# A second copy of the first weight, loaded in 2 KB pieces, for the first 16 batches of a conditional adapter

## The chip, the cores and the metric

The kernel runs on one core of one Trainium2 chip. The metric is the time of one launch on the device, in microseconds (us), as the median of several runs. A profile of one further execution stands beside it.

## What is computed

`x` is 128 batches of 128 x 512 float32. Every batch has an id that picks one of ten sets of adapter weights: W1 (512 x 128), b1, W2 (128 x 512), b2, gamma and beta. The reference, cut to what matters:

```python
w1 = W1[language_ids]; w2 = W2[language_ids]
h = relu(einsum('bsh,bha->bsa', x, w1) + b1[ids][:, None, :])
adapted = einsum('bsa,bah->bsh', h, w2) + b2[ids][:, None, :]
y = x + adapted
normed = (y - mean(y)) * rsqrt(var(y) + 1e-5)          # over the last axis, 512
out = x + normed * gamma[ids][:, None, :] + beta[ids][:, None, :]
```

## The kernel before

All ten W1 and all ten W2 are loaded into SBUF once (2.62 MB each) and stay there; a batch picks its own by a register that holds its id. `x` comes in groups of four batches (`load_x`, 1 MB, four buffers), results leave in pairs (`store`, 512 KB). All large transfers are issued by SyncE (SP) in one order; an instruction that waits holds up those behind it on SP. Every engine's order is written out by hand: `keep` ties each instruction to the one before it on its engine.

One batch `b` takes these steps:

- `transpose_x(b)` (L199): four TensorE transposes turn the 128 x 512 block into four 128 x 128 blocks in PSUM. Column block `k` of `x` holds the 128 consecutive columns from `k * 128`. The block of `x` is the stationary operand of the transpose, so it is read by the weight load (LDWEIGHTS, "PEld" in the profile); the identity matrix streams past it.
- `copy_xT(b)` (L204): ScalarE (ACT) copies the result to SBUF.
- `stage_w1(b)` (L194): ACT copies the batch's W1 from the resident table `w1` to a small buffer `w1s`[...].
- `down(b)` (L221): four matmuls, each over 128 of the 512 columns, give h transposed in the one PSUM buffer `ph`; they show as eight records.
- `relu(b)` (L231): ACT adds b1, applies relu and writes `hT`; it frees `ph` for `down(b + 1)`.
- `up(b)` (L235): a matmul with W2, 512 wide, into one of five PSUM buffers `py`. For batches 0 to 3 and some others one more matmul (L241) adds b2 there.
- VectorE (DVE) adds x (`residual`) and later scales (`scale`, `finish`), ACT squares and takes the deviation, GpSimd (POOL) forms x + b2 (`add_b2`, tile `r`) and x + beta (`add_beta`, tile `o`, five pair buffers).

In the main loop TensorE does, for each `i`, `transpose_x(i)`, `down(i - 1)`, `up(i - 2)`.

Ahead of that loop stands a start-up. SP issues: the ids, gamma, x of batches 0 and 1 (`load_part`, L84), W1 in four transfers (L98), x of batches 2 and 3, W2 in two transfers (L103), x of batches 4 to 7 in two, then groups 2 and 3 (`load_x`, L67). Each of the four W1 transfers brings the rows of one column block `k` of all ten sets: to a partition go ten separate pieces of 128 floats, 512 bytes each. W2 and `x` come in 2 KB pieces.

Meanwhile thirty rows (ten each of beta, gamma, b2) are spread over all partitions: `spread(r)` is a matmul on TensorE (L163) and a copy of its result from PSUM by DVE (L168) or ACT (L166), even rows on DVE and odd ones on ACT. Rows 0 to 23 come before the first `stage_w1`; rows 24 to 29 come in a loop over the first four batches (called the four-batch loop here), which also holds `down(0)` to `down(3)`, `transpose_x(2)` and `(3)`, the relus, and `stage_w1(2)` to `(5)`. `spin` is filler work on TensorE. After the four-batch loop come `up(0)` and `up(1)`, the first use of W2.

Of the kernel before, what the change touches and what calls it, by code (L numbers as in the profile page):

```python
# [8 lines left out]
FP = mybir.dt.float32  # L9
# [4 lines left out]
ET = mybir.EngineType  # L14
PSUM = bass.MemoryType.PSUM

P = 128
G = 4
EPS = 1e-5
U = 2  # L20


@with_exitstack
def cond_resid_kernel(ctx: ExitStack, tc: tile.TileContext, x, itok, W1, b1, W2, b2, gamma, beta, out):
# [8 lines left out]
    nc = tc.nc  # L33
    B, S, H = x.shape
    L, _, A = W1.shape
    KC = H // P
# [6 lines left out]
    def keep(ins):  # L43

        engine = ins.ins.engine
        if engine in last:
            tc.add_manual_dep(ins.ins, last[engine], behind, reason="kept order")
        last[engine] = ins.ins.name
        return ins

    const = ctx.enter_context(tc.tile_pool(name="const", bufs=1))
# [13 lines left out]
    def load_x(g):  # L65
        t = xp.tile([P, G, H], FP, tag="x", name=f"x_{g}")
        keep(nc.sync.dma_start(out=t, in_=x[g * G : (g + 1) * G].rearrange("b s h -> s b h")))  # L67
        xs[g] = t

    def xb(b):  # L70
        return xs[b // G][:, b % G, :]
# [3 lines left out]
    rows = rp.tile([P, H], FP, tag="r", name="rows")  # L75
    b1r = const.tile([L, A], FP, name="b1r")
    w1 = const.tile([P, L, KC, A], FP, name="w1")
    w2 = const.tile([P, L * H], FP, name="w2")
    x_0 = xp.tile([P, G, H], FP, tag="x", name="x_0")
    xs[0] = x_0  # L80

    def load_part(lo, hi):
        dst = xs[lo // G][:, lo % G : lo % G + hi - lo, :]
        keep(nc.sync.dma_start(out=dst, in_=x[lo:hi].rearrange("b s h -> s b h")))  # L84
# [8 lines left out]
    warm = const.tile([P, 1], FP, name="warm")  # L93
    keep(nc.vector.memset(warm, 1.0))
    keep(nc.scalar.activation(warm, warm, AF.Sqrt))
    for k in range(KC):
        keep(
            nc.sync.dma_start(out=w1[:, :, k, :], in_=W1[:, k * P : (k + 1) * P, :].rearrange("l p a -> p l a"))  # L98
        )
    load_part(2, G)  # L100
    for l in range(0, L, 5):
        keep(
            nc.sync.dma_start(  # L103
                out=w2[:, l * H : (l + 5) * H].rearrange("p (l h) -> p l h", l=5),
                in_=W2[l : l + 5].rearrange("l a h -> a l h"),
# [3 lines left out]
    xs[1] = x_1  # L109
    load_part(G, G + 2)  # L110
    load_part(G + 2, 2 * G)
    for g in range(2, 4):
        load_x(g)

    ident = const.tile([P, P], FP, name="ident")
    make_identity(nc, ident)
    eps = const.tile([P, 1], FP, name="eps")
    nc.gpsimd.memset(eps, EPS)
    ones = const.tile([P, P], BF, name="ones")
# [4 lines left out]
    R = 3 * L  # L124
# [34 lines left out]
    def spread(r, copier):  # L159
        t = (beta_b, gamma_b, b2_b)[r // L]  # L160
        row = p_y.tile([P, H], FP, tag="y", name=f"row_{r}")
        pick_r = pick[:, r : r + 1].to_broadcast([96, P])
        keep(nc.tensor.matmul(row, lhsT=pick_r, rhs=parts[:96, :], start=True, stop=True))  # L163
        dst = t[:, r % L * H : (r % L + 1) * H]
        if copier is nc.scalar:
            keep(nc.scalar.copy(dst, row))  # L166
        else:
            keep(nc.vector.tensor_copy(dst, row))  # L168

    lids, xT, w1s, hT, rs, os, ys, ssqs, nmeans, rstds = {}, {}, {}, {}, {}, {}, {}, {}, {}, {}  # L170
    phs, pxs, sums = {}, {}, {}

    def lid(b, engine):
        g = b // G
        if (g, engine) not in lids:
            loads, vals = nc.values_load_multi_w_load_instructions(
                lang[0:1, g * G : (g + 1) * G],
                engines=[engine],
                min_val=0,
                max_val=L - 1,  # L180
                skip_runtime_bounds_check_because="clamped on the chip to 0..L-1 above",
            )
            for ins in loads:
                keep(ins)
            lids[g, engine] = vals
        return lids[g, engine][b % G]
# [6 lines left out]

    def stage_w1(b):  # L194
        w1s[b] = wp.tile([P, KC, A], FP, tag="w1s", name=f"w1s_{b}")
        src = w1.rearrange("p l k a -> p (l k a)")[:, bass.ds(lid(b, ET.Activation) * (KC * A), KC * A)]
        keep(nc.scalar.copy(w1s[b].rearrange("p k a -> p (k a)"), src))  # L197

    def transpose_x(b):  # L199
        pxs[b] = p_x.tile([P, KC, P], FP, tag="xT", name=f"pxT_{b}")  # L200
        for k in range(KC):
            keep(nc.tensor.transpose(pxs[b][:, k, :], xb(b)[:, k * P : (k + 1) * P], ident))  # L202

    def copy_xT(b):  # L204
        xT[b] = tp.tile([P, KC, P], FP, tag="xT", name=f"xT_{b}")
        keep(nc.scalar.copy(xT[b], pxs.pop(b)))  # L206
# [14 lines left out]
    def down(b):  # L221
        phs[b] = p_h.tile([P, P], FP, tag="h", name=f"ph_{b}")
        for k in range(KC):
            keep(
                nc.tensor.matmul(  # L225
                    phs[b], lhsT=w1s[b][:, k, :], rhs=xT[b][:, k, :], start=(k == 0), stop=(k == KC - 1)
                )
            )
        del xT[b], w1s[b]

    def relu(b):  # L231
        hT[b] = tp.tile([P, P], FP, tag="hT", name=f"hT_{b}", bufs=6)
        keep(nc.scalar.activation(hT[b], phs.pop(b), AF.Relu, bias=b1T[:, bass.ds(lid(b, ET.Activation), 1)]))  # L233
# [53 lines left out]
    def rstd_1(g):  # L287
        y0s[g] = p_s.tile([P, 6], FP, tag="s", name=f"stat_{g}")
        keep(nc.vector.reciprocal(y0s[g][:, 0:2], sds[g]))  # L289

    def rstd_2(g):
        t = y0s[g]
        keep(nc.vector.scalar_tensor_tensor(t[:, 2:4], ssqs.pop(g), EPS * H3, t[:, 0:2], ALU.add, ALU.mult))

# [27 lines left out]
    def on(b):  # L322
        return 0 <= b < B
# [6 lines left out]
    def rstd_of(b, n):  # L330
# [6 lines left out]
        elif n == 2:  # L337
            keep(
                nc.vector.scalar_tensor_tensor(t[:, 1:2], ssqs.pop(b), EPS * H3, t[:, 0:1], ALU.add, ALU.mult)
            )  # L340
# [94 lines left out]
    def spin(n, width):  # L435
        idle = p_s.tile([P, H], FP, tag="s", name="idle")
        for _ in range(n):
            keep(
                nc.tensor.matmul(
                    idle[:, :width], lhsT=ones, rhs=ones[:, 0:1].to_broadcast([P, width]), start=True, stop=True  # L440
                )
            )


    def spread_turn(lo, hi):
        for r in range(lo, hi):
            spread(r, nc.scalar if r % 2 == 1 else nc.vector)
            if r % 2 == 1:
                spin(1, H // 2)
# [6 lines left out]
    spread_turn(2, 8)  # L456
    transpose_x(1)
    copy_xT(1)
    spread_turn(8, 24)
    stage_w1(0)  # L460
    stage_w1(1)
    spin(3, H)
    for b in range(4):
        down(b)
        if b < 2:
            transpose_x(b + 2)
        relu(b)
        if b < 2:
            copy_xT(b + 2)
        for r in range(24 + 2 * b, min(26 + 2 * b, R)):  # L470
            spread(r, nc.scalar if r % 2 == 1 else nc.vector)
        stage_w1(b + 2)
    up(0)
    up(1)

    for i in range(3, B + U):
        b = i - U - 1
        if b > 0 and b % G == 0 and b // G + 3 < NG:
            load_x(b // G + 3)
        if i == 4:  # L480
            up(2)
        if i == 5:
            up(3)
        if i > 3 and on(i):
            transpose_x(i)
        if b <= E:
            add_b2(b + 2)
            add_beta(b)
        if i > 4 and on(i - 1):
            down(i - 1)  # L490
        if i > 3 and on(i):
            copy_xT(i)
        if i > 4 and on(i + 1):
            stage_w1(i + 1)
        if i > 4 and on(i - 1):
            relu(i - 1)
        if i > 5 and on(i - U):
            up(i - U)


        g, half = divmod(b, 2)
        p = g - 1
        mine, old = 0 <= p < B // 2, 0 <= p - 1 < B // 2
        if b == E:
            add_b2(b + 3)
            add_beta(b + 1)
            add_b2(b + 4)
            for n in range(b + 2, B):
                add_beta(n)
        if b > E:  # L510
            tail(b)
        elif half == 0:
            if on(b):
                residual(b)
            if mine:
                rstd_1(p)
                scale(2 * p)
            if on(b):
                negative_mean(b)
            if mine:  # L520
                rstd_2(p)
            if old:
                finish(2 * p - 1)
                store(p - 1)
            if mine:
                rstd_3(p)
        else:
            if on(b):
                residual(b)
            if mine:  # L530
                rstd_4(p)
                scale(2 * p + 1)
            if on(b):
                negative_mean(b)
            if mine:
                finish(2 * p)
        if 0 <= b <= E:
            square(b)
            if half == 1:
                deviation(g)  # L540

        for n, engine in ((i + 3, ET.Activation), (i - U + 3, ET.PE), (b + 1, ET.DVE), (b + 5, ET.Pool)):
            if on(n):
                lid(n, engine)
# [37 lines left out]
```

## Time and profile before

| quantity | value |
|---|---|
| median of 3 runs | 314.34 us (314.3 to 314.67) |
| the profiled execution's own time | 314.2 us |
| its span in the profile | 312.4 us |
| TensorE (PE) busy | 300.3 us, 96% |
| DVE, ACT, POOL busy | 295.6, 285.8, 280.1 us |
| moved by DMA | 72.87 MB, 233 GB/s over the span |

The span runs from the first to the last instruction of the program; 1.8 us of the execution's time lie outside it. "Busy" is the time in which an engine has an instruction in flight. In the tables of the profile a group is named by line, engine, operation and tiles (output first, then inputs), and "issue" is time in which an engine waited for nothing that the profile shows. The 40 slices are 7.8 us each; a digit is the busy share in tenths.

### The profile page before, as it was taken

The numbers are of one execution on the slowest core, as the hardware profiler recorded it, in microseconds if no ns is written. First come the engines' busy times: TensorE is split into PE (matmuls) and PEld (weight loads), VectorE is DVE, ScalarE is ACT, GpSimd is POOL, SyncE is SP. The second block draws the span as 40 slices with busy tenths as digits, with TensorE's granted clock in tenths as the row PEclk, the third lists the DMA queues.
The fourth block names the chain that finished last, engine by engine and source line by source line (L and its number), as shares of the span: only waits on it lengthen the run. The fifth ranks groups of instructions, "written<-read, shape, count | busy, mean of one in ns | idle before, by whom it ended". The sixth has DMA issues, their size and how long they took to land.

```text
span 312.4 us, 7096 instructions
## 1 busy us (share of the span) xinstructions
PE 300.3 (96%) x1870; PEld 222.8 (71%) x1871; DVE 295.6 (95%) x943; ACT 285.8 (91%) x726; POOL 280.1 (90%) x234
## 2 busy tenths in 40 slices
PE   8999999999999999999999999999999999999980
PEld 3566777777777777777777777777777777777740
DVE  6827999999999999999999999999999999999995
ACT  3977999999999999999999999999999999999982
POOL 1307999999999999999999999999999999999964
PEclk9999999999999999999999999999999999999995
DMA  7998678677766667677666667787666667733244
GB/s 208 315 387 317 202 263 271 227 247 269 245 228 234 219 229 266 203 270 270 229 218 213 232 250 244 234 273 268 212 214 213 245 235 236 265 134 129 78 167 168
DMA packets 41001, 72.87 MB, mean 233 GB/s; under 512 B 1753, under 2 KB 6884, under 8 KB 40962
## 3 DMA queue, kind: packets, MB, share of 16 engines
q1 hardware_dynamic: 40902, 72.38, 67.2%
q8 instruction: 15, 0.25, 0.3%
q14 instruction: 24, 0.20, 0.2%
q10 hardware_dynamic: 60, 0.05, 0.1%
HBM read 38.86 MB, written 33.55 MB: 232 GB/s over the span
## 4 chain that ended last, share of the span: by engine, by line
PE 84%; DVE 4%; DMA 4%; SPq 3%; ACT 2%; issue 1%; DVEq 1%; ACTq 0%
PE ph L225 34%; PE py L242 33%; PE pxT L202 17%; DMA w<-in_L_cond_W_dram 4%; SPq L98 2%; PE py L241 1%; DVE py L257 1%; DVE py L306 1%; SPq L84 1%; DVE o L315 1%; ACT sq L350 0%; DVEq L577 0%; ACT xT L206 0%; ACT n L366 0%; ACT sq L272 0%
## 5 line engine op out<-in xcount | busy, mean ns | idle before, releaser
L219 POOL TENSOR_TENSOR o<-x,beta_b 128x512 f32<-128x512 f32 x128 | 162.2, 1280 | 9.1 <-ACT beta_b L166 9.1
L225 PE MATMUL ph<-xT,w1s 128*128 128x128 f32 x1024 | 135.6, 275 | 0.8 <-ACT w1s L197 0.5
L212 POOL TENSOR_TENSOR r<-x,b_b 128x512 f32<-128x512 f32 x93 | 118.9, 1279 | 15.9 <-DMA x<-in_x_dram 11.9
L242 PE MATMUL py<-w,hT 128*128 x256 | 131.2, 594 | 0.5 <-DMA w<-in_L_cond_W_dram 0.5
L225 PEld LDWEIGHTS ph<-xT,w1s 128*128 128x128 f32 x1024 | 124.6, 192 | 3.0 <-ACT hT L233 1.6
L202 PEld LDWEIGHTS pxT<-ident,x 128*128 128x128 f32 x512 | 63.7, 141 | 65.1 <-issue 45.9
L306 DVE SCALAR_TENSOR_TENSOR py<-py,nmean,gamma_b 128x512 f32<-128x512 f32 x126 | 93.6, 743 | 0.0
L315 DVE SCALAR_TENSOR_TENSOR o<-py,rstd,o 128x512 f32<-128x512 f32 x122 | 90.8, 745 | 0.0
L272 ACT ACTIVATE sq<-py,sum 128x512 f32<-128x512 f32 x124 | 85.2, 687 | 2.0 <-DVE py L257 1.8
L206 ACT COPY xT<-pxT 128x512 f32<-128x512 f32 x128 | 73.7, 576 | 9.4 <-PE pxT L202 5.8
L197 ACT COPY w1s<-w 128x512 f32 x128 | 79.3, 620 | 0.2 <-issue 0.2
L202 PE MATMUL pxT<-ident,x 128*128 128x128 f32 x512 | 76.8, 273 | 0.0
L257 DVE SCALAR_TENSOR_TENSOR py<-py,r 128x512 f32<-128x512 f32 x93 | 64.4, 693 | 1.4 <-issue 0.5
L233 ACT ACTIVATE hT<-ph,b1T 128x128 f32<-128x128 f32 x128 | 47.3, 370 | 1.2 <-PE ph L225 1.2
L242 PEld LDWEIGHTS py<-w,hT 128*128 128x128 f32 x256 | 40.5, 192 | 3.2 <-issue 1.6
L257 DVE SCALAR_TENSOR_TENSOR py<-py,x 128x512 f32<-128x512 f32 x35 | 24.3, 695 | 3.8 <-PE py L242 3.3
L272 ACT ACTIVATION_READ_ACCUMULATOR sq<-py,sum 128x1 f32 x124 | 25.6, 207 | 0.0
L283 ACT ACTIVATE sd<-ssq,eps 128x2 f32<-128x2 f32 x62 | 18.3, 296 | 2.1
L263 DVE TENSOR_SCALAR nmean<-sum 128x1 f32<-128x1 f32 x128 | 19.4, 151 | 0.1
L289 DVE RECIPROCAL stat<-sd 128x2 f32<-128x2 f32 x62 | 12.9, 208 | 1.1 <-ACT sd L283 1.1
L257 DVE DVE_READ_ACCUMULATOR py<-py,r 128x1 f32 x93 | 13.3, 143 | 0.0
L301 DVE RECIPROCAL rstd<-stat 128x2 f32<-128x2 f32 x62 | 10.3, 167 | 0.0
(55 smaller groups left out, 111.2 us busy)
## 6 DMA issues: line engine op xcount, KB each, us to landing
out_dram<-o SPq DMA_DIRECT2D x61, 512.0 KB, 3.2
x<-in_x_dram SPq DMA_DIRECT2D x30, 1024.0 KB, 6.0
w<-in_L_cond_W_dram SPq DMA_DIRECT2D x4, 640.0 KB, 6.3
w<-in_L_cond_W_dram SPq DMA_DIRECT2D x2, 1280.0 KB, 11.3
x<-in_x_dram SPq DMA_DIRECT2D x4, 512.0 KB, 8.2
out_dram<-o SPq DMA_DIRECT2D x6, 256.0 KB, 2.0
rows<-in_L_cond_beta_dram ACTq DMA_DIRECT2D x1, 20.0 KB
rows<-in_L_cond_gamma_dram SPq DMA_DIRECT2D x1, 20.0 KB
```

The costliest lines, as they stand in the source:

```text
L197: keep(nc.scalar.copy(w1s[b].rearrange("p k a -> p (k a)"), src))
L202: keep(nc.tensor.transpose(pxs[b][:, k, :], xb(b)[:, k * P : (k + 1) * P], ident))
L206: keep(nc.scalar.copy(xT[b], pxs.pop(b)))
L212: keep(nc.gpsimd.tensor_tensor(rs[b], xb(b), b2_b[:, bass.ds(v * H, H)], ALU.add))
L219: keep(nc.gpsimd.tensor_tensor(os[g][:, j, :], xb(b), beta_b[:, bass.ds(v * H, H)], ALU.add))
L225: nc.tensor.matmul(phs[b], lhsT=w1s[b][:, k, :], rhs=xT[b][:, k, :], start=(k == 0), stop=(k == KC - 1))
L233: keep(nc.scalar.activation(hT[b], phs.pop(b), AF.Relu, bias=b1T[:, bass.ds(lid(b, ET.Activation), 1)]))
L242: keep(nc.tensor.matmul(ys[b], lhsT=hT[b], rhs=w2[:, bass.ds(v * H, H)], start=not m, stop=True))
L257: nc.vector.scalar_tensor_tensor(ys[b], ys[b], 1.0, r, ALU.mult, ALU.add, accum_out=col(sums, b))
L272: nc.scalar.activation(sq, ys[b], AF.Square, bias=col(sums, b), scale=-float(H), accum_out=col(ssqs, b))
L306: nc.vector.scalar_tensor_tensor(ys[b], ys[b], col(nmeans, b), gamma_b[:, bass.ds(v * H, H)], ALU.add, ALU.mult)
L315: nc.vector.scalar_tensor_tensor(o, ys.pop(b), rstds[g][:, j : j + 1], o, ALU.mult, ALU.add)
```

## The change

A second table `w1e` holds all ten W1 in another order: partition `p` takes the four consecutive rows `4p` to `4p + 3` of W1, so that one set is one piece of 2 KB for a partition. It is loaded in two transfers where the four of W1 stood. Batches 0 to 15 take their W1 from it. For the sum over columns to match, their transposes take for block `k` the columns `k, k + 4, k + 8, ...` of `x`: 128 floats at a step of four (16 bytes). The usual `w1` is still loaded, as four transfers in 512-byte pieces, one each in iterations 4, 6, 8 and 10 of the main loop, and serves batches 16 to 127. The load of group 3 of `x` moves from the start-up into iteration 5. Of the thirty rows, 20 instead of 24 are spread ahead of the first `stage_w1`; in the four-batch loop come three a batch instead of two, of which the one with `r % 3 == 1` is copied by ACT and the others by DVE.

```diff
+EARLY = 16
...
     w1 = const.tile([P, L, KC, A], FP, name="w1")
+    w1e = const.tile([P, L, KC, A], FP, name="w1e")
...
-    for k in range(KC):
+    for l in range(0, L, 5):
+        keep(
+            nc.sync.dma_start(
+                out=w1e[:, l : l + 5].rearrange("p l k a -> p l (k a)"),
+                in_=W1[l : l + 5].rearrange("l (p k) a -> p l (k a)", k=KC),
+            )
+        )
+    load_part(2, G)
+
+    def load_w1(k):
         keep(
             nc.sync.dma_start(out=w1[:, :, k, :], in_=W1[:, k * P : (k + 1) * P, :].rearrange("l p a -> p l a"))
         )
-    load_part(2, G)
...
-    for g in range(2, 4):
-        load_x(g)
+    load_x(2)
...
     def stage_w1(b):
-        src = w1.rearrange("p l k a -> p (l k a)")[:, bass.ds(lid(b, ET.Activation) * (KC * A), KC * A)]
+        src = (w1e if b < EARLY else w1).rearrange("p l k a -> p (l k a)")[:, bass.ds(lid(b, ET.Activation) * (KC * A), KC * A)]
...
     def transpose_x(b):
         for k in range(KC):
-            keep(nc.tensor.transpose(pxs[b][:, k, :], xb(b)[:, k * P : (k + 1) * P], ident))
+            if b < EARLY:
+                cols = xb(b).rearrange("s (p k) -> s k p", k=KC)[:, k, :]
+            else:
+                cols = xb(b)[:, k * P : (k + 1) * P]
+            keep(nc.tensor.transpose(pxs[b][:, k, :], cols, ident))
...
-    spread_turn(8, 24)
+    spread_turn(8, 20)
...
-        for r in range(24 + 2 * b, min(26 + 2 * b, R)):
-            spread(r, nc.scalar if r % 2 == 1 else nc.vector)
+        for r in range(20 + 3 * b, min(23 + 3 * b, R)):
+            spread(r, nc.scalar if r % 3 == 1 else nc.vector)
...
+        if i == 5:
+            load_x(3)
+        if i in (4, 6, 8, 10):
+            load_w1((i - 4) // 2)
```

On SP the order becomes: ids, gamma, x 0-1, the two of `w1e`, x 2-3, the two of W2, x 4-5, x 6-7, group 2, `load_w1(0)`, group 3, `load_w1(1)`, group 4, `load_w1(2)`, `load_w1(3)`, the first store, group 5, and on as before. Up to group 4 nothing but `group 4` waits for a compute engine; the transfers share eight semaphores in turn, so each also waits for the one eight places ahead of it to have landed.

## The prediction

> **What bounds the kernel now.** I read the page first: the share of each engine, the DMA slices, and the chain that ended last.
>
> ```profile
> PE 300.3 (96%) x1870; PEld 222.8 (71%) x1871; DVE 295.6 (95%) x943; ACT 285.8 (91%) x726; POOL 280.1 (90%) x234
> ...
> DMA  7998678677766667677666667787666667733244
> ...
> PE 84%; DVE 4%; DMA 4%; SPq 3%; ACT 2%; issue 1%; DVEq 1%; ACTq 0%
> PE ph L225 34%; PE py L242 33%; PE pxT L202 17%; DMA w<-in_L_cond_W_dram 4%; SPq L98 2%; PE py L241 1%; DVE py L257 1%; DVE py L306 1%; SPq L84 1%; DVE o L315 1%; ACT sq L350 0%; DVEq L577 0%; ACT xT L206 0%; ACT n L366 0%; ACT sq L272 0%
> ```
>
> The chain is TensorE for 84%, and the only large rest is a DMA of weights (4%) with its issue on SP. The chain in order of time, in its first 45 us, says where that is:
>
> ```profile
> 10.48 0.47 SPq L103
> 10.95 0.04 issue
> 10.99 11.29 DMA w<-in_L_cond_W_dram
> 22.28 0.14 issue
> 22.41 1.10 PE py L242 x2
> ```
>
> The last byte of W2 lands at 22.28, and `up(0)` starts at 22.41. From there to 300 us the chain is nearly all TensorE, so a microsecond gained or lost at 22.41 reaches the end, and so does each nanosecond added to TensorE's own work. The timeline of PE and ACT shows how near the next limit is:
>
> ```profile
> 13.12 1.13 ACT L166 COPY b_b<-row 128x512 f32<-128x512 f32 x2
> 14.47 1.14 ACT L197 COPY w1s<-w 128x512 f32 x2 [0.23 <-issue]
> ```
>
> ```profile
> 15.14 1.16 PE L225 MATMUL ph<-xT,w1s 128*128 128x128 f32 x8 [0.54 <-ACT w1s L197]
> ...
> 20.51 1.16 PE L225 MATMUL ph<-xT,w1s 128*128 128x128 f32 x8 [0.17 <-ACT hT L233]
> 21.50 0.38 PE L241 MATMUL py<-parts,pick 96*128 96x512 bf16 x1
> 22.41 1.10 PE L242 MATMUL py<-w,hT 128*128 x2 [0.53 <-DMA w<-in_L_cond_W_dram]
> ```
>
> The other chain to `up(0)` is: ACT ends its row copies at 14.25, stages W1 at 14.47, `down(0)` starts at 15.14, the four-batch loop ends, and `up(0)` could have gone on at about 21.72 (its b2 matmul at 21.50 and 0.22 for it, the gap seen between 23.35 and 23.57 in `up(1)`). W2 costs only 0.7 us beyond that: an earlier W2 is worth nothing more unless this chain moves too. W1's last piece landed at 14.15 by the landing records, 0.1 before ACT was free: both were equally late.
>
> Last the busy time by stage (columns: PE, PEld, DVE, ACT, POOL, granted clock, DMA share, GB/s):
>
> ```profile
> 8.00:12.00 4.00, 4.00 (x26) 2.35 (x25) 3.81 (x7) 4.00 (x8) 1.43 (x2) 1.00 1.20 290
> 14.00:18.00 4.00, 3.40 (x25) 2.79 (x25) 1.20 (x2) 2.92 (x7) 0.00 (x0) 1.00 1.05 386
> 36.00:40.00 4.00, 4.00 (x27) 2.95 (x26) 4.00 (x14) 3.88 (x11) 4.00 (x5) 1.00 0.21 37
> ```
>
> While W1 comes, DMA moves 290 GB/s; with 2 KB pieces 386. Later it has gaps (37 GB/s at 36 to 40).
>
> **The change, part by part.**
>
> *W1 in 2 KB pieces.* By packet records a 512-byte packet of W1 took 34 ns, a 2 KB one 88 ns. W1 is 5120 of the former, 16 at a time: it landed from 4.95 (x 0-1 there) to 14.15, 9.2 us. In 2 KB pieces it is as long as W2, whose halves landed at 18.90 and 22.28, 3.38 each: 6.8 us. So `w1e` lands at about 11.7 and all behind it 2.4 earlier: W2 at 19.9, x 4-5 at about 22.5 instead of 24.86. [...]
>
> *Four rows fewer ahead of the first stage.* ACT drops two copies at 0.565 each (1.13 for two): free at 13.12, `stage_w1(0)` at 13.35. `w1e` is there 1.6 us earlier, so no wait takes the place. `down(0)` at about 14.0 to 14.05, 1.1 earlier. DVE's copies end as much earlier.
>
> *Three rows a batch in the four-batch loop.* One matmul more in each of the first three batches and one in the fourth (row 29), 0.22 each. ACT still copies one row in each of three batches, DVE two of 0.69 (1.4 in a cycle of about 1.8, and it has nothing else). Followed through: `down(1)` starts 0.2 later after `down(0)` than before; ACT's relus, copies and stages then come 0.9 to 0.7 earlier than before; `down(3)` at 19.85 (before 20.51); row 29; the b2 matmul of `up(0)` at about 21.05; W2's own at 21.3. W2 has been there since 19.9. So `up(0)` starts at 21.3 instead of 22.41: **1.1 us gained**. Less than the 2.4 of the DMA, because the four-batch loop is then the last to end. What comes next (`transpose_x(4)` at 25.50) needs x 4-5, which moves more than PE does; the ACT chain of 26 to 29 follows its input, with the same instructions in the same order. POOL's first `add_b2`, which waited 11.95 us for x 4-5, starts earlier too.
>
> *The second load of W1 and the moved group 3.* I follow SP's queue at before's rates (512-byte transfers 2.26 each, a group of x 2.7, a store 1.35): group 2 lands at 25.4 to 26.6, W1(0) 27.7, group 3 30.4 (before 31.56), W1(1) 32.6, group 4 35.3, W1(2) 37.6, W1(3) 39.8, first store 41.2. Group 3 is first used near 41, group 4 and W1 near 50: cost nothing, covered by these slacks. Issuing W1(2) and (3) keeps SP [...], and the first store, which went out at 33.70, lands 5 to 6 us later than now. Behind that store waits POOL's `add_beta(10)`, which reuses the first pair buffer; it ran at 43.49, so about 42.4 now. About 1 us of margin, then the second store (45) before `add_beta(12)` (47.2, then 46.1). If it is missed, POOL stalls; but `r` of batch 10 ended at 38.6 and DVE took it at 44.82, so 6 us of lead cover it. Zero, with an upper end of 2.
>
> *x at a step of four.* This is what the trace does not show: no weight load in it reads at a step. Its normal pace, in a batch of the steady state:
>
> ```profile
> 101.91 0.14 PEld L202 LDWEIGHTS pxT<-ident,x 128*128 128x128 f32 x1 [0.24 <-ACT w1s L197]
> 102.34 0.36 PEld L202 LDWEIGHTS pxT<-ident,x 128*128 128x128 f32 x3 [0.29 <-issue]
> 102.67 0.97 PEld L225 LDWEIGHTS ph<-xT,w1s 128*128 128x128 f32 x8
> ```
>
> The first of four loads is done under `up`; the other three go at 110 ns (0.33 to the next line's start), as do the matmuls, so a slower load is paid in full. PE's batch is 4 x 110 + 8 x 111 + 2 x 430 = 2.19 us, the period that the timeline shows: no slack. Of the 16 batches, 0 and 1 are transposed in the start-up under row copies; 14 pay, with three loads each, 42 loads. The lower end is zero: a step makes no less to read. [...] If it doubles, 42 x 110 ns = 4.6 us lost and the sum is +3.5; if free, -1.1. I take near zero, because the load is slow as it is: 110 ns for 128 columns is 0.86 ns an element, while a bf16 matmul of 512 columns passes in 0.22 us, 0.42 ns an element[...]. This is an argument, not a row, so the upper end stays in the range. Break-even is 1.1 us / 42 = 26 ns a load.
>
> **Sum.** 314.2 (profiled) - 1.1 + 0 + 0 = 313.1; the median before stands 0.14 above that execution, so 313.2.
>
> **The rivals.**
> 1. *Strided loads cost PE more than the start gains.* For it: PE without slack, load and matmul equally long[...]. Against: the slow pace of float32. Half as long again (55 ns) gives 42 x 55 = 2.3, so 315.5; doubled 317.7; it decides from 26 ns a load. This is the one on the other side.
> 2. *A small cost, 11 to 41 ns a load.* 0.5 to 1.7 us lost (42 loads) against 1.1 gained: 313.7 to 314.9, no change.
> 3. *The four-batch loop or the DMA gives nothing.* If `w1e` comes no faster, W2 still sets `up(0)`: 314.3. Against it: 290 and 386 GB/s.
> 4. *Late stores stall POOL beyond its lead.* 1 to 2 us lost, about 315. Against it: 6 us of lead.
>
> **How the numbers follow.** Main case 0.48 (312.7 to 313.6); small cost 0.10 and rival 3 0.05: no change; rival 1 0.32, rival 4 0.05. A measurement of this kernel can tell about 0.2%, 0.6 us, from no change. Faster 0.48, same 0.15, slower 0.37. The range takes in rival 1 to the doubling: 312.6 to 318.0; outside are a load of more than double length and a gain beyond 1.7.
>
> **What would show it.** W1 at about 386 GB/s by 12 us and no DMA wait at `up(0)`; `stage_w1(0)` near 13.4, `up(0)` with W2 near 21.3; the weight loads of the transposes 110 ns apart in batches 4 to 15, and batch periods of 2.19 there. Wrong if those periods are longer than the later ones (2.5 if doubled), if PE waits for `w1s` at 14, or if POOL waits for a store near 43.

## The result and the profile after

The changed kernel took 313.82 us (median of 22 runs, 313.62 to 314.48) against 314.34 before: the ratio is 0.9979, with a 95% interval of 0.9972 to 0.9985. That is 0.5 us faster, with an interval that does not reach 1, in the direction forecast and at half the size; it is also less than the 0.6 us that the forecast took as the least that can be told from no change. In a second set of runs on one chip (the run `e12_after` below) it was 313.80 against 314.27, ratio 0.9987 (0.9980 to 0.9994).

The page of the changed kernel, shares of the engines, the DMA slices and the chain that ended last:

```profile
PE 300.5 (96%) x1869; PEld 223.8 (72%) x1869; DVE 297.3 (95%) x945; ACT 285.4 (91%) x724; POOL 280.1 (90%) x234
...
DMA  6999998767776777667666567576666667633234
...
PE 91%; DVE 5%; ACT 1%; issue 1%; DVEq 1%; DMA 1%; ACTq 0%
PE ph L241 36%; PE py L258 34%; PE pxT L218 18%; PE py L257 1%; PE row L175 1%; DVE py L273 1%; DVE gamma_b L180 1%; DVE py L322 1%; DVE o L331 1%; DMA rows<-in_L_cond_b_dram 1%; ACT sq L366 0%; DVEq L597 0%; ACT n L382 0%; DVE left L156 0%; DVE left L154 0%
```

The DMA of weights has left the chain: PE holds 91% of it instead of 84%, and rows and copies (L175, L180) fill the start. The start-up in the timeline of ACT and then PE:

```profile
13.37 1.14 ACT L209 COPY w1s<-w1e 128x512 f32 x2 [0.15 <-DVE gamma_b L180]
```

```profile
14.04 1.16 PE L241 MATMUL ph<-xT,w1s 128*128 128x128 f32 x8 [0.47 <-ACT w1s L209]
...
19.81 1.16 PE L241 MATMUL ph<-xT,w1s 128*128 128x128 f32 x8
20.80 0.38 PE L175 MATMUL row<-parts,pick 96*128 96x512 bf16 x1
21.02 0.38 PE L257 MATMUL py<-parts,pick 96*128 96x512 bf16 x1
21.24 1.02 PE L258 MATMUL py<-w,hT 128*128 x2
```

Stage, `down(0)`, `down(3)` and `up(0)` stand 1.1, 1.1, 0.7 and 1.17 us earlier than before, and the last line has no wait for a DMA any more. The busy time by stage shows W1 coming faster than before's 290 GB/s, and before's empty stretch at 36 to 40 filled by the second load:

```profile
8.00:12.00 4.00, 4.00 (x25) 2.35 (x24) 3.77 (x7) 4.00 (x8) 1.37 (x2) 1.00 1.04 376
36.00:40.00 4.00, 4.00 (x27) 3.09 (x26) 3.93 (x15) 3.83 (x11) 4.00 (x4) 1.00 1.19 302
```

So 1.17 us were won at `up(0)` and 0.5 arrived. Six places in the traces show where the rest went (us from the span's start; "t" is the first transpose of a batch on PE). The second profile of the changed kernel stands beside the first.

| | `up(0)` | t(4) | t(16) | t(127) | end of DVE's work | end of span |
|---|---|---|---|---|---|---|
| before | 22.41 | 25.50 | 51.12 | 297.75 | 309.49 | 312.44 |
| changed | 21.24 | 24.26 | 50.18 | 296.99 | 308.74 | 312.07 |
| changed, second profile | 21.22 | 24.24 | 50.16 | 296.77 | 308.52 | 311.86 |
| lead of the second profile | 1.19 | 1.26 | 0.96 | 0.98 | 0.97 | 0.58 |

The lead shrinks in two places: by 0.30 between batches 4 and 16, and by 0.39 after the last work is done. The first profile differs from the second by stalls of 0.16 to 0.19 us on PE that occur in single batches: one in batch 44, which the second profile does not have, makes up most of the 0.2 us between them. One in batch 74 stands in both and one in batch 26 is found before only, so these cancel. What the stalls are is left open.

### The profile page after: what moved, and what is told of

The parts are those of the page before. It is cut to its first block, busy times and chain, and to the rows that moved or that the text cites. A ratio compares the mean times of both kernels' runs of the same rounds, so it can differ in the third digit from the quotient of the medians.

```text
span 312.1 us, 7096 instructions
## 1 busy us (share of the span) xinstructions
PE 300.5 (96%) x1869; PEld 223.8 (72%) x1869; DVE 297.3 (95%) x945; ACT 285.4 (91%) x724; POOL 280.1 (90%) x234
## 2 busy tenths in 40 slices
DMA packets 42313, 75.49 MB, mean 242 GB/s; under 512 B 1785, under 2 KB 6916, under 8 KB 42274
## 4 chain that ended last, share of the span: by engine, by line
PE 91%; DVE 5%; ACT 1%; issue 1%; DVEq 1%; DMA 1%; ACTq 0%
PE ph L241 36%; PE py L258 34%; PE pxT L218 18%; PE py L257 1%; PE row L175 1%; DVE py L273 1%; DVE gamma_b L180 1%; DVE py L322 1%; DVE o L331 1%; DMA rows<-in_L_cond_b_dram 1%; ACT sq L366 0%; DVEq L597 0%; ACT n L382 0%; DVE left L156 0%; DVE left L154 0%
## 5 line engine op out<-in xcount | busy, mean ns | idle before, releaser
L218 PEld LDWEIGHTS pxT<-ident,x 128*128 128x128 f32 x512 | 65.5, 148 | 64.9 <-issue 44.8
L209 ACT COPY w1s<-w 128x512 f32 x112 | 69.5, 621 | 0.0
```

The source lines that it names most:

```text
L218: keep(nc.tensor.transpose(pxs[b][:, k, :], cols, ident))
```

## The experiments

**The step without the rest: `e1_plain`.**

```diff
-                cols = xb(b).rearrange("s (p k) -> s k p", k=KC)[:, k, :]
+                cols = xb(b)[:, k * P : (k + 1) * P]
```

> The changed kernel with one thing undone: the transposes of batches 0 to 15 read 128 consecutive columns again, while W1 still comes from w1e, so the sum over columns is not the reference's in those 16 batches. Theory (the step costs little): in the trace of the changed kernel PE's lead over before shrinks from 1.25 us at the transposes of batch 4 to 0.94 us at those of batch 16, 0.03 us a batch. Without the step the lead should stay at 1.2 to 1.25 us, each batch period be 2.19 us instead of 2.22, and the time be 0.3 us below the changed kernel's, about 313.5. Rival (the step costs nothing; the shrinking lead comes from the second load of W1, which runs at the same time): periods stay 2.22 and the time 313.8.

Measured: t(4) at 24.25, as in the changed kernel; t(16) at 49.86 against 50.18; periods of 2.19 in batches 8 to 15. 313.46 us, ratio to before 0.9976 (0.9966 to 0.9985). PE's lines of it in the same stretch, and then those of the changed kernel:

```profile
34.31 0.60 PE L218 MATMUL pxT<-ident,x 128*128 128x128 f32 x4
34.74 1.06 PE L241 MATMUL ph<-xT,w1s 128*128 128x128 f32 x8
35.64 1.02 PE L258 MATMUL py<-w,hT 128*128 x2
36.50 0.60 PE L218 MATMUL pxT<-ident,x 128*128 128x128 f32 x4
```

```profile
34.41 0.63 PE L218 MATMUL pxT<-ident,x 128*128 128x128 f32 x4
34.88 1.06 PE L241 MATMUL ph<-xT,w1s 128*128 128x128 f32 x8
35.78 1.02 PE L258 MATMUL py<-w,hT 128*128 x2
36.64 0.63 PE L218 MATMUL pxT<-ident,x 128*128 128x128 f32 x4
```

From the transposes to `down` it is 0.47 us with the step and 0.43 to 0.44 without; all else is equal. With the second load of W1 running in both, the step alone is the loss of 0.3 us. The intervals of the two times overlap; it is the traces that tell them apart.

**The step in all batches: `e2_all`.**

```diff
-EARLY = 16
+EARLY = 128
...
-        if i in (4, 6, 8, 10):
-            load_w1((i - 4) // 2)
```

> The step and w1e in all 128 batches, and no second load of W1: the output is the reference's. If the step costs 0.026 to 0.03 us a batch, 124 batches pay 3.2 to 3.7 us against a gain of 1.2 at the start: 316.3 to 316.9, with every batch period 2.22 (2.44 with b2 on PE). If instead the second load makes the periods longer, periods are 2.19 throughout and the time is about 313.1.

Measured: 316.67 us, ratio 1.0086 (1.0073 to 1.0099), periods 2.22 and 2.44 to the end. From `up(0)` (21.30) to PE's last matmul (304.77) it is 3.39 us longer than before (22.41 to 302.49): 0.027 us for each of 124 batches. The small cost of the first theory is confirmed over 124 batches instead of 12, and without any second load.

**No second load of W1: `e3_noload`.**

```diff
-        src = (w1e if b < EARLY else w1).rearrange(...)
+        src = w1e.rearrange(...)
...
-        if i in (4, 6, 8, 10):
-            load_w1((i - 4) // 2)
```

> The changed kernel without the second load of W1: all batches take W1 from w1e, but only batches 0 to 15 read x at a step of four, so the sum is not the reference's from batch 16 on. Theory (the second load lies in gaps of the DMA and costs nothing): the same time as the changed kernel, 313.8, and up(0), the transposes of batches 4 and 16 at the same places as there (21.2, 24.3, 50.2). Rival (it costs some tenths, by late x, late stores[...]): 0.2 to 0.4 us below, 313.5.

Measured: 313.50 us, ratio 0.9982 (0.9975 to 0.9988): the rival's number. But the places are those of the changed kernel: t(4) 24.36, t(16) 50.28, t(127) 296.88, end of DVE's work 308.62. The second load costs PE nothing. The difference arises after all work, from there to the end of the span: 3.08 us here, 3.33 in the changed kernel, 2.95 before. That is taken up under "The order of the last waits" below.

In the changed kernel the second load did reach POOL. Its timeline:

```profile
39.60 1.26 POOL L228 TENSOR_TENSOR r<-x,b_b 128x512 f32<-128x512 f32 x1
43.12 2.51 POOL L235 TENSOR_TENSOR o<-x,beta_b 128x512 f32<-128x512 f32 x2 [2.25 <-DMA out_dram<-o]
45.59 1.28 POOL L228 TENSOR_TENSOR r<-x,b_b 128x512 f32<-128x512 f32 x1
48.25 1.28 POOL L235 TENSOR_TENSOR o<-x,beta_b 128x512 f32<-128x512 f32 x1 [1.39 <-DMA out_dram<-o]
```

`add_beta(10)` and `(12)` waited 2.25 and 1.39 us for stores that were late. POOL's lead over DVE covered both, as the equal t(16) and t(127) of `e3_noload` show.

**The rows alone, and the loads alone: `e4_rows` and `e5_oldrows`.** The first puts the new order of rows into the kernel before; the second puts the old order into the changed kernel:

```diff
-    spread_turn(8, 24)
+    spread_turn(8, 20)
...
-        for r in range(24 + 2 * b, min(26 + 2 * b, R)):
-            spread(r, nc.scalar if r % 2 == 1 else nc.vector)
+        for r in range(20 + 3 * b, min(23 + 3 * b, R)):
+            spread(r, nc.scalar if r % 3 == 1 else nc.vector)
```

> The kernel before with the rows alone moved: 20 rows ahead of the first stage_w1, three a batch after it. W1 in 512-byte pieces lands at 14.15, so the first stage_w1 can't move from 14.4, and W2 lands at 22.28 as before. Theory (the rows are worth something only with the faster load): down(0) at about 15.1, up(0) at 22.4, 314.3 (same). Rival (the rows alone bring the gain): down(0) at 14.0, up(0) near 21.3 to 22.4, up to 1 us faster.

Measured: 314.30 us, ratio 1.0007 (1.0001 to 1.0014). `down(0)` stays at 15.14 and `up(0)` comes at 22.66, held by W2. One line of ACT, then PE:

```profile
14.47 1.14 ACT L197 COPY w1s<-w 128x512 f32 x2 [0.76 <-DMA w<-in_L_cond_W_dram]
```

```profile
15.14 1.16 PE L225 MATMUL ph<-xT,w1s 128*128 128x128 f32 x8 [1.07 <-ACT w1s L197]
...
22.66 0.67 PE L242 MATMUL py<-w,hT 128*128 x1 [0.24 <-DMA w<-in_L_cond_W_dram]
```

The wait ahead of `down(0)` has grown from 0.54 to 1.07: ACT was free earlier, and W1 was not there, so ACT's first stage waited 0.76 us for it.

> The changed kernel with the rows as before: 24 ahead of the first stage_w1, then two a batch. W1 and W2 come early, but ACT's copies hold the first stage_w1 to 14.4. Theory (two chains, DMA and the four-batch loop, end at up(0) nearly together, so that the load alone brings only the 0.7 us by which W2 was later than the loop): up(0) at 21.7, less 0.3 for the step, so 0.2 to 0.4 us faster than before, about 314.0. Rival (the DMA was the only bound): up(0) near 20 to 21, as fast as the changed kernel or faster.

Measured: `down(0)` at 15.33, `up(0)` at 21.98, 0.43 earlier than before; t(16) only 0.19 earlier, after the step. 314.34 us, ratio 1.0002 (0.9993 to 1.0010): no gain, where 0.2 to 0.4 had been expected. The end of the span took 3.34 us here too, which the expectation did not count. In this profile ACT's first row copy came 0.17 late (6.71 against 6.53 before), ahead of anything that the edit touches, so by an estimate (0.43 + 0.17) the loads alone are worth nearer 0.6 us at `up(0)`. Neither part alone changes the time, but for two reasons: the rows leave `up(0)` waiting for W2, while the loads do move it, and the step (0.3) and the later end (0.38) take that back. The two together move it by 1.17.

**The order of the last waits: `e9_two` and `e10_lanes`.** By the landing records of both kernels the transfers of a kernel share eight semaphores in turn. After the last instruction SP waits for all of them, in the same order in every trace of this case (seven instructions, about 0.063 us apart: in the changed kernel they start from 310.85 to 311.22). Before, the last store falls on the semaphore that this order asks for last; in the changed kernel, with two transfers more, on the one that it asks for first. The waits of SP's queue in the last microseconds (waiting line, what for, us in total, times, longest), before and then after:

```profile
SPq L577 <- DMA out_dram<-o: 1.3, 2, 0.6
```

```profile
SPq L597 <- DMA out_dram<-o: 1.7, 1, 1.7
```

Before, SP works through the others while the stores are still under way; after, it sits 1.7 us at the first and then has six more ahead of it: 6 x 0.063 = 0.38 us, the size of the loss. The last store itself is no slower: 2.05 us from issue to landing before (309.52 to 311.57) and 2.06 after (308.77 to 310.83). From its landing to the end of the span it is 0.87 us before and 1.24 after. `e3_noload` is a place between them: its last store falls on the semaphore with two waits behind it, and there it is 0.98. Two experiments change the number of transfers.

```diff
# e9_two, against the changed kernel
-            nc.sync.dma_start(out=w1[:, :, k, :], in_=W1[:, k * P : (k + 1) * P, :].rearrange("l p a -> p l a"))
+            nc.sync.dma_start(
+                out=w1[:, 5 * k : 5 * k + 5].rearrange("p l k a -> p (l k) a"),
+                in_=W1[5 * k : 5 * k + 5].rearrange("l (k p) a -> p (l k) a", p=P),
+            )
...
-        if i in (4, 6, 8, 10):
-            load_w1((i - 4) // 2)
+        if i in (4, 8):
+            load_w1((i - 4) // 4)
```

> The changed kernel with the second load of W1 in two transfers (five sets each) instead of four, in iterations 4 and 8, same bytes and pieces; the output is the reference's. The number of transfers is then that of the kernel before. Theory (the end waits for the eight DMA semaphores in a fixed order, and the last store falls on the first of them in the changed kernel and on the last of them before, which costs six waits of 0.063 us): from the end of DVE's last instruction to the end of the span 2.95 us instead of 3.33, the time 0.38 below the changed kernel's, near 313.45. Rival (the longer end is a slower landing of the last store, chance): 3.3 us and 313.8.

```diff
# e10_lanes, against the kernel before
     for g in range(2, 4):
-        load_x(g)
+        xs[g] = xp.tile([P, G, H], FP, tag="x", name=f"x_{g}")
+        load_part(g * G, g * G + 2)
+        load_part(g * G + 2, g * G + 4)
```

> The kernel before with the loads of groups 2 and 3 of x in two halves each, so two transfers more, and nothing else; the output is the reference's. Theory (order of the final waits): 3.33 us instead of 2.95 from DVE's end to the end of the span, 0.38 slower than before, about 314.6. Rival (chance): no change.

Measured: from the end of DVE's work to the end of the span 2.97 us in `e9_two` and 3.32 in `e10_lanes`, with the waits turned round (first `e9_two`, then `e10_lanes`):

```profile
SPq L600 <- DMA out_dram<-o: 1.2, 2, 0.6
```

```profile
SPq L579 <- DMA out_dram<-o: 1.7, 1, 1.7
```

The times follow on the same chip: `e9_two` 313.42 us (seven runs, 313.24 to 313.58), ratio to before 0.9972 (0.9960 to 0.9983), 0.38 below the changed kernel's 313.80; `e10_lanes` 314.65, 0.38 above before's 314.27, ratio 1.0010 (1.0001 to 1.0018). The theory holds in both directions, and `e9_two` beats both kernels. In the profile of `e9_two` W2 landed at 21.34, 0.5 later than in the changed kernel, and `up(0)` came at 21.48; that profile took 313.58, so the gain of 0.38 rests on the medians and on the end of the span.

`e10_lanes` is the cleaner of the two, since `e9_two` changes one thing more, against its expectation: in its trace the packets of the second load are 2 KB, each filled from four 512-byte pieces of W1 (38441 packets in all, against 42313 in the changed kernel). They took 116 to 124 ns, those of `x` 84 to 88, and W1 came no faster for it: 294 GB/s from 38 to 40 us, where the changed kernel with its 512-byte packets moves 306. So a 2 KB packet alone did not bring the faster rate here.

**The changed kernel again: `e12_after`.**

> The changed kernel itself, for a comparison with the one of two transfers on one chip, and for a second profile. up(0) at 21.2, periods of 2.22 in batches 4 to 15, 3.33 us at the end; the single stalls of about 0.16 us on PE in batches 44 and 74 should be elsewhere or not there at all if they are chance, and in the same batches if the program causes them.

Measured: 313.80 us; `up(0)` at 21.22, periods of 2.22, 3.34 us at the end. The stall in batch 44 is gone, the one in batch 74 is there again; it is also in `e9_two`, `e1_plain`, `e3_noload` and `e4_rows`, but not in `e8_rows18`. So it is not pure chance, and its cause is open.

**Other steps: `e6_step2`, `e11_step8`, `e7_step16`.** The kernel before with another step in the transposes, and nothing else changed:

```diff
# e6_step2, all batches
-            keep(nc.tensor.transpose(pxs[b][:, k, :], xb(b)[:, k * P : (k + 1) * P], ident))
+            cols = xb(b).rearrange("s (q p t) -> s q t p", q=2, t=2)[:, k // 2, k % 2, :]
+            keep(nc.tensor.transpose(pxs[b][:, k, :], cols, ident))
# e7_step16, from batch 8 on
+                cols = xs[b // G].rearrange("s b h -> s (b h)").rearrange("s (p t) -> s t p", t=16)[:, b % G * KC + k, :]
# e11_step8, from batch 8 on, pair = the batch and its neighbour as one row
+                cols = pair.rearrange("s (p t) -> s t p", t=8)[:, b % 2 * KC + k, :]
```

> The kernel before with the transposes of all batches reading x at a step of two (8 bytes[...]); the columns of the blocks are other ones, so the sum is not the reference's. W1, DMA and order are untouched. Theory A [...]: periods 2.19, time 314.3. Theory B (the cost grows with the step): between nothing and the step of four's 0.03 us a batch, so up to 2 us slower.

> The kernel before with the transposes of batches 8 to 127 reading x at a step of sixteen (64 bytes, over the four batches of a group; the sum is not the reference's). Theory A [...]: the same cost as the step of four, periods 2.22, 120 x 0.03 = 3.6 us slower, 317.9. Theory B (the cost grows with the step): clearly more, 5 us and up. A weight load is then 0.2 us long in the record, as at a step of four, or longer.

> The kernel before with the transposes of batches 8 to 127 reading x at a step of eight (32 bytes, over pairs of batches; the sum is not the reference's). Steps of two and four cost 0.03 us a batch, a step of sixteen 0.01. If the cost falls with the step, this lies between, 0.01 to 0.03 us a batch (315.4 to 317.9). If steps below the 64 bytes of sixteen all cost the same, 0.03 us a batch: 317.6 to 317.9. [...]

Measured: the step of two 317.70 us (ratio 1.0110, 1.0095 to 1.0126), the step of eight 314.51 (1.0006, 0.9997 to 1.0014), the step of sixteen 315.44 (1.0039, 1.0025 to 1.0053). The weight loads of the transposes between 66 and 290 us, in this order: before, the step of two, of four (`e2_all`), of eight, of sixteen (count, shortest, median and longest record in ns, first and last start):

```profile
L202 PEld LDWEIGHTS pxT<-ident,x x404: 137/141/143, 66.2 to 289.0; 128*128 128x128 f32 x135
```

```profile
L203 PEld LDWEIGHTS pxT<-ident,x x399: 195/196/209, 66.8 to 290.0; 128*128 128x128 f32 x200
```

```profile
L218 PEld LDWEIGHTS pxT<-ident,x x399: 195/206/209, 66.0 to 288.9; 128*128 128x128 f32 x200
```

```profile
L206 PEld LDWEIGHTS pxT<-ident,x x404: 185/188/192, 66.3 to 289.1; 128*128 128x128 f32 x135
```

```profile
L205 PEld LDWEIGHTS pxT<-ident,x x401: 188/190/196, 66.9 to 289.7; 128*128 128x128 f32 x134
```

Every step makes the record about 50 to 65 ns longer, but moves the starts far less. On PE the four transposes of a batch and the `down` behind them start 109 ns apart without a step; with a step of two or four the gaps are 109, 116 to 117, 120 and 120, with sixteen 109, 111, 113 and 114, with eight 109 three times and then 111 (medians). The usual batch period is 2.19 us without a step, 2.22 with two and four, 2.19 (in a few batches 2.20) with eight, 2.20 with sixteen. The theories fall: the step of two costs as much as the step of four (2.22 us a batch with either), the larger steps cost less (2.19 with eight, 2.20 with sixteen), and the step of eight costs less than was put down for it (314.51 us against 315.4 to 317.9). `e6_step2` and `e7_step16` also had `down(0)` 0.5 and 0.2 us later than before, so the periods are the cleaner measure.

**Two rows fewer still: `e8_rows18`.**

```diff
-    spread_turn(8, 20)
+    spread_turn(8, 18)
...
-        for r in range(20 + 3 * b, min(23 + 3 * b, R)):
-            spread(r, nc.scalar if r % 3 == 1 else nc.vector)
+        for r in range(18 + 3 * b, min(21 + 3 * b, R)):
+            spread(r, nc.scalar if r % 3 == 2 else nc.vector)
```

> A version that may beat both: the changed kernel with 18 rows ahead of the first stage_w1 and three in each of the first four batches, the third copied by ACT. w1e lands at 12.7 and ACT is then free at 12.3, so the first stage_w1 starts at 12.7 to 12.8 instead of 13.37. W2 landed at 20.8, 0.4 before up(0). Theory (the four-batch loop bounds up(0), the loads follow closely): up(0) at 21.0 to 21.2, hardly earlier, since two more matmuls stand in the fourth batch and W2 lands at 20.8: 0 to 0.3 us below the changed kernel. Rival: the loop's ACT chain gets no shorter and the rows of the fourth batch delay up(0): 0.2 us slower than the changed kernel.

Measured: 313.61 us, ratio 0.9981 (0.9974 to 0.9987), not to be told from the changed kernel. The profile is no clean one for the question: the first row copy on ACT came at 6.93 us, 0.42 later than in the changed kernel (6.51), before anything that the edit touches. The first stage at 13.24 and `up(0)` at 21.53 carry that delay; the three rows of the fourth batch stand on PE between `down(3)` (19.67) and `up(0)`, as the rival said. The experiment is inconclusive: if there is a gain, it is too small for these times.

## Why the prediction was right, and where it was mis-sized

The gain at the start came by the path that the forecast gave. The stated range, 312.6 to 318.0, holds 313.82, but it was made wide for a doubled weight load, which was the author's estimate. The main case, 312.7 to 313.6, does not hold it, and by the forecast's own 0.6 us the result is no change, which it gave 0.15. The number lies in the second rival's 313.7 to 314.9, and that is luck in part: the step alone would have left 314.34 - 1.19 - 0.07 + 0.30 = 313.4, in the main case, and the rest is a cost at the end that no case had. Of the forecast's own signs of being wrong, longer periods in batches 4 to 15 and a wait of POOL for a store near 43 did come; PE's wait of 0.47 us for `w1s` at 14 came too, but lies in the forecast's own start of `down(0)` at 14.0.

- *Two chains end at `up(0)`; the four-batch loop would be the next bound.* Right. Forecast: stage at 13.35, `down(0)` at 14.0, `down(3)` at 19.85, `up(0)` at 21.3; measured 13.37, 14.04, 19.81 and 21.24. `e4_rows` and `e5_oldrows` show both chains: with the rows alone W2 held `up(0)`, with the loads alone ACT's row copies and the loop behind them did.
- *W1 in 2 KB pieces.* Right in kind, too large in size: `w1e` landed at 12.7 instead of 11.7, W2 at 20.8 instead of 19.9 (landing records). From 8 to 12 us it came at 376 GB/s (before, in 512-byte pieces, 290), not 386, which is the smaller part; from 5 to 6 us only 266 GB/s were moved and from 7 to 8 us 330, and why is open. The forecast's 34 ns for a 512-byte packet is 32 to 33 in the records. W2 was still 0.4 us ahead of `up(0)`, since the loop was later, but the margin is small: in the profile of `e9_two` W2 held it again.
- *The second load costs nothing.* Right for PE, by `e3_noload`. The margin given for the stores was wrong: the first store landed at about 43, not 41.2, so POOL did wait; the lead of 6 us named in the forecast is what held.
- *x at a step of four: zero taken.* This term was mis-sized: 0.027 us a batch, 0.30 us in batches 4 to 15. It was the small cost that the second rival had, just below its range of 11 to 41 ns a load: 0.30 us over the 36 loads of those twelve batches, three each, is 8 ns. The doubling in the first rival did appear in part, in the record of the load (141 to about 200 ns), and the sum did not follow it, because the starts moved by at most 11 ns (to 120 ns apart, against 109). The forecast's reason for taking near zero, the slow pace of a float32 load (0.86 ns an element against 0.42 in a bf16 matmul), was the author's argument, and no run shows it: what was measured is a small cost, 3.39 us over the 124 batches of `e2_all`, and the step of two has the same batch period, 2.22 us.
- *The end of the span.* A term left out of the sum, 0.38 us: two more transfers move the last store to the semaphore that is waited for first. `e9_two` and `e10_lanes` show it. The forecast counted each moved transfer on SP and in the queue, and not how many there are in all.

The sum, by the second profile: -1.19 at `up(0)`, -0.07 up to t(4), +0.30 for the step, -0.01 in the rest, +0.39 at the end: -0.58, which is the profiled execution's 313.62 against 314.2.

## What to carry to other kernels

Where two chains end together, find both before moving one: here the rows alone did not bring `up(0)` forward, the loads alone by 0.4 us, and the two together by 1.2. A change in the number of transfers can move the end of a kernel through the order of the final waits (here by 0.38 us); compare the time from the last work to the end of the span in both profiles before you look for a loss in the loop. Judge an operand's access by the starts of the instructions that follow one another, not by the length of their records: here the records grew by about 60 ns (141 to about 200) and the starts moved by at most 11 (109 to 120).

## What the runs showed of the hardware

- A float32 weight load of 128 columns at a step of two or four elements had a record of 196 to 206 ns (`e6_step2`, `e2_all`; medians) instead of 141 and made a batch of four transposes 0.03 us longer; at a step of eight or sixteen (`e11_step8`, `e7_step16`) the record was 188 to 190 ns and the batch at most 0.01 us longer. That wider steps cost less was not forecast, and its cause is open.
- The final waits on DMA semaphores took about 0.063 us each, and only those counted that stood behind the one of the last store: 0.38 us between the best and the worst place (0.87 us from landing to end with none behind in the kernel before, 0.98 with two in `e3_noload`, 1.24 with six in the changed kernel).
- While W1 came in 2 KB pieces, DMA moved 376 GB/s (changed kernel, 8 to 12 us), in 512-byte pieces 290 (before, 8 to 12 us); with 2 KB packets filled from 512-byte pieces it moved 294 (`e9_two`, 38 to 40 us).
